# Seeding PSUM banks with ScalarE copies in the last layer of a two-layer transformer kernel

## The chip, the cores and the metric

One NeuronCore of a Trainium2 chip. The metric is the device time of one launch, in microseconds (us), of the slowest core, which here is the only one. TensorE multiplies matrices into PSUM (eight banks of 128 partitions by 512 float32). VectorE (DVE in the profile) and ScalarE (ACT) read and write PSUM and SBUF. GpSimd (POOL) works here on SBUF alone. The engines run in parallel, each through its own instruction stream in order, and wait for each other by semaphores.

## The reference

32 sequences of 128 tokens with 512 channels go through two layers. Layer 0 is attention with 16 heads of 64 and a mixture of eight experts. Layer 1, which the change concerns, is this:

```
normed = adaln(x, cond, w_adaln1, b_adaln1)          # layer norm, scale and shift from cond
q, k, v = normed @ wq.T + bq, normed @ wk.T + bk, normed @ wv.T + bv      # 16 heads of 32
attn = softmax(where(mask, -inf, q @ k.T / sqrt(32)))
x = x + (attn @ v) @ wo.T + bo
normed = adaln(x, cond, w_adaln2, b_adaln2)
h = gelu(normed @ w1.T + b1)                          # 512 -> 2048
x = x + h @ w2.T + b2                                 # 2048 -> 512
```

All in float32; shapes: x (32, 128, 512), wq, wk, wv, wo (512, 512), w1 (2048, 512), w2 (512, 2048).

## The kernel before

**Order of the work.** The kernel does not write its instructions in a fixed order. Every operation is handed to `Sched.op` (line 147) with an engine, a planned duration, a priority, the buffers that it reads and writes, and sometimes a second engine that could do it (`also`). `Sched.run` (line 193) then plans all engines together: it takes the operation that would leave its engine idle least, then the one of lowest priority number, and so fixes each engine's order once and for all when the program is built. The planned durations are in the functions at lines 299 to 316: 0.88 us for a product of the last layer, 0.68 us for a VectorE sum over 512 columns, 1.13 us for one on GpSimd, 0.62 us for a ScalarE copy. The helper `tt` (line 1199) hands in a sum of two tensors; unless its last argument is False, the planner may give it to VectorE (line 1201) or to GpSimd (line 1202).

**Seven products for eight.** All matrix products of layer 1 are done in Winograd's form of Strassen's algorithm: both operands are cut into quarters, seven products P1 to P7 of sums of quarters are made, and the four blocks of the result are

```
U2 = P1 + P6      U3 = U2 + P7      U4 = U2 + P5
C11 = P1 + P2     C12 = U4 + P3     C21 = U3 + P4     C22 = U3 + P5
```

The kernel works on groups of two sequences (`group`, line 2414) and on pairs G of groups (eight of them). In `group`, the q and k products (lines 2438 to 2481) write each of the seven P into a bank of its own; VectorE makes U2, U3, U4 and the four blocks from them, 512 columns at a time, and ScalarE takes P1 out of PSUM. The products for v and for the attention's output do the same in `seven_T` (line 2484) with 256 columns; the output's results are added to the residual x by VectorE (`onto_x`, `out_x`).

**The two levels of the MLP.** `up` (line 2667) makes h for a pair G and `down` (line 2742) the second product. Here the form is used twice: seven outer products in the order `ORDER` = 1, 2, 6, 7, 5, 4, 3, each made by seven inner ones in `inner` (line 2627). An inner product is four matmuls over 128x128 tiles. `inner` holds four banks: X collects P1, then P6, then P7 by accumulation, and ScalarE copies X out after each (`snap`, line 2641); Y takes P2, W takes P4, Z takes P5 and then P3. VectorE makes the four blocks with one sum each (`comb`, line 2645). Products of `up` carry m in the tile's name and those of `down` n, with the pair's number and the bank's letter: `m_3z` is bank Z of an inner product of `up` for G = 3.

In `up`, the outer sums U2, U3, U4 and the blocks of h are then made in SBUF by `add` (line 2684), four sums of 512 columns for each of the outer products 2, 6, 7, 4 and 3 and eight for 5, on either engine. Blocks of h go through the gelu on ScalarE (line 2693). In `down`, `form` and `sums` (line 2788) make the sums of quarters of h that the products need: 16 and 28 of 512 columns for each G, on either engine. They and the copies of the weights' pieces (`piece`, line 2617, on SyncE's queue) run ahead of the products by gates on `inner_done` and `stream`. The attention of the next two groups is planned in between the MLP of a pair.

**PSUM banks.** `bank` (line 342) is a new tile of the pool for each use; the planner counts eight.

Of the kernel before, what the change touches and what calls it, by code (L numbers as in the profile page):

```python
# [19 lines left out]
P = 128  # L20
# [30 lines left out]
class Buf:  # L51
# [3 lines left out]
    __slots__ = ("cls", "shape", "dtype", "name", "tile", "left", "end", "writers", "readers", "view")  # L55

    def __init__(self, cls, shape, dtype, name, tile=None):
        self.cls, self.shape, self.dtype, self.name, self.tile = cls, shape, dtype, name, tile
        self.left, self.end = 0, 0.0
        self.writers, self.readers = {}, {}  # L60
# [29 lines left out]
class Views:  # L90
# [36 lines left out]
    def give(self, at, b):  # L127
        self.free.append((at, b.view))

# [189 lines left out]
class Stage:  # L319


    def __init__(self, nc, ctx, tc, name, window, rows, smls, weights):
# [8 lines left out]
        self.views = Views(self.rows, self.weights)  # L331

# [9 lines left out]
    def bank(self, name, shape=(P, D)):  # L342
        return Buf(self.banks, list(shape), F32, name)

# [741 lines left out]
def fast_kernel(ctx: ExitStack, tc: tile.TileContext, x, condT, mask, cols, w_ada, wqkv, wout, wout_p, wout_o, wgate,  # L1086
# [86 lines left out]
    def transpose4(dst, src):  # L1173
        for c in range(4):
            nc.tensor.transpose(dst[:, c * P : (c + 1) * P], src[:, c * P : (c + 1) * P], ident)  # L1175
# [1158 lines left out]
    row = st.view  # L2334
# [26 lines left out]
    for i in (1, 2):  # L2361
# [7 lines left out]
    spun1 = bank("spun1")  # L2369
    sch.op(PE, 2.4, lambda: spin(22, spun1.t), w=[spun1], r=[pb0], prio=LB - 820.5, job=LJ)  # L2370

    dbq = const_tile("dbq", (P, 2))
    dbq_b = stands(dbq)
    sch.op(DVE, 0.16, lambda: nc.vector.tensor_tensor(
        dbq, prm[:, COL["bq"] + 2 : COL["bq"] + 4], prm[:, COL["bq"] : COL["bq"] + 2], ALU.subtract), w=[dbq_b], prio=900, job=5)
# [38 lines left out]
    def group(g):  # L2414
# [23 lines left out]
        ps = {m: bank(f"qk{m}_{g}", (P, 2, 2, S)) for m in range(1, 8)}  # L2438
        U1, U2, U3, U4 = (row(f"qu{m}_{g}", (P, 2, 2, S)) for m in "1234")

        def prod_qk(m, what, rhs, rr, ps=ps):
            for z, n in enumerate("qk"):
                w_, wb = l1w[n + what]

                def f_(z=z, w_=w_):
                    for u in range(2):
                        for k in range(2):
                            nc.tensor.matmul(ps[m].t[:, z, u, :], w_()[:, k, u * P : (u + 1) * P], rhs()[:, k, :],
                                             start=(k == 0), stop=(k == 1))
                sch.op(PE, mm_us(S, 4), f_, w=[(ps[m], z)], r=rr + [wb], prio=pp, job=job, keep=3)  # L2450

        def comb_qk(o_, a_, m, ps=ps):
            sch.op(DVE, dve_us(D), lambda: nc.vector.tensor_tensor(o_.t, a_.t, ps[m].t, ALU.add), w=[o_], r=[a_, ps[m]],
                   prio=pp, job=job)

        def first_qk(U1=U1, X=ps[1]):
            for u in range(2):
                nc.scalar.activation(U1.t[:, 0, u, :], X.t[:, 0, u, :], AF.Identity, bias=col("bq", u), scale=1.0)
            nc.scalar.copy(U1.t[:, 1, :, :], X.t[:, 1, :, :])

        def third_qk(U2=U2, U3=U3, X=ps[7]):
            for u in range(2):
                nc.vector.scalar_tensor_tensor(U3.t[:, 0, u, :], X.t[:, 0, u, :], dbq[:, u : u + 1], U2.t[:, 0, u, :],
                                               ALU.add, ALU.add)
            nc.vector.tensor_tensor(U3.t[:, 1, :, :], U2.t[:, 1, :, :], X.t[:, 1, :, :], ALU.add)

        prod_qk(1, "11", lambda: N_(1, 1), rN(1, 1))
        sch.op(ACT, 2 * act_us(S, 1) + act_us(QD), first_qk, w=[U1], r=[ps[1]], prio=pp - 1, job=job)
        prod_qk(2, "12", lambda: N_(2, 1), rN(2, 1))
        comb_qk(qk[1, 1], U1, 2)  # L2470
        prod_qk(6, "s2", lambda: NTv(2), [NTn[2]])
        comb_qk(U2, U1, 6)
        prod_qk(7, "s3", lambda: NTv(3), [NTn[3]])
        sch.op(DVE, 2 * dve_us(S, 1) + dve_us(QD), third_qk, w=[U3], r=[U2, ps[7], dbq_b], prio=pp, job=job)
        prod_qk(5, "s1", lambda: NTv(1), [NTn[1]])
        comb_qk(qk[2, 2], U3, 5)
        comb_qk(U4, U2, 5)
        prod_qk(4, "22", lambda: NTv(4), [NTn[4]])
        comb_qk(qk[2, 1], U3, 4)
        prod_qk(3, "s4", lambda: N_(2, 2), rN(2, 2))  # L2480
        comb_qk(qk[1, 2], U4, 3)
        v = [row(f"v_{g}_{i}") for i in range(GB)]

        def seven_T(n, Bn, rB, Tv, Tn, pr, first, comb, out2):

            ps = {m: bank(f"{n}{m}_{g}", (P, QD)) for m in range(1, 8)}
            U = {m: row(f"{n}u{m}_{g}", (P, QD)) for m in range(1, 5)}

            def prod(m, what, lhs, rr):
                w_, wb = l1w[n + what]  # L2490

                def f_():
                    for k in range(2):
                        nc.tensor.matmul(ps[m].t, lhs()[:, k, :], w_()[:, k, :], start=(k == 0), stop=(k == 1))
                sch.op(PE, mm_us(QD, 2), f_, w=[ps[m]], r=rr + [wb], prio=pr, job=job, keep=3)

            prod(1, "11", lambda: Bn(1, 1), rB(1, 1))
            sch.op(ACT, act_us(QD), lambda: nc.scalar.copy(U[1].t, ps[1].t), w=[U[1]], r=[ps[1]], prio=pr - 1, job=job)
            first(U[1], [(1, 1)])
            prod(2, "12", lambda: Bn(2, 1), rB(2, 1))  # L2500
            out2(1, 1, U[1], ps[2])
            prod(3, "s4", lambda: Bn(2, 2), rB(2, 2))
# [429 lines left out]
```

## Time and profile before

| what | value |
|---|---|
| three runs | 3350.45, 3350.43, 3348.22 us; median 3350.43 us |
| the profiled execution | 3349.9 us, span 3348.1 us, mean granted TensorE clock 0.983 |
| busy in the span | TensorE 3165.6 us (95%), VectorE 2642.0 (79%), GpSimd 1262.1 (38%), ScalarE 1060.6 (32%) |
| layer 1 | about 1907 us to the end |
| one pair G of layer 1 | 175.8 us from the first product of `down` of one G to that of the next |

The profile's page gives busy time by engine, the span in 40 slices and the costliest groups of instructions. Its rows name tiles as out<-in; `base` is a piece of a shared SBUF tile, so that most operands of layer 1 go by that name and must be told apart by line and shape. A float32 matmul shows as two records. The figure after `|` in a group's row is the engine's idle time just before the group and what ended it. A TensorE shown as busy is not one at its peak, since the records' ends are modelled; the distance from one start to the next tells the rate.

### The profile page before, as it was taken

The numbers are of one execution on the slowest core, as the hardware profiler recorded it, in microseconds if no ns is written. First come the engines' busy times: TensorE is split into PE (matmuls) and PEld (weight loads), VectorE is DVE, ScalarE is ACT, GpSimd is POOL, SyncE is SP. The second block draws the span as 40 slices with busy tenths as digits, with TensorE's granted clock in tenths as the row PEclk, the third lists the DMA queues.
The fourth block names the chain that finished last, engine by engine and source line by source line (L and its number), as shares of the span: only waits on it lengthen the run. The fifth ranks groups of instructions, "written<-read, shape, count | busy, mean of one in ns | idle before, by whom it ended". The sixth has DMA issues, their size and how long they took to land. (4 is left out here: it accounts for less than half of the span.)

```text
span 3348.1 us, 60612 instructions
## 1 busy us (share of the span) xinstructions
PE 3165.6 (95%) x22740; PEld 2563.1 (77%) x22740; DVE 2642.0 (79%) x5217; ACT 1060.6 (32%) x2613; POOL 1262.1 (38%) x939
## 2 busy tenths in 40 slices
PE   9999999999999999999999999898989898989887
PEld 5555555555568888888888898797979788888877
DVE  8877776888878876677555388888989888888887
ACT  3323332344330221222212124333333334342432
POOL 0322222221030456677665204334242515161625
PEclk9999999999999999999999999999999999999989
DMA  4243323453145433334333516445463535463655
GB/s 168 98 141 119 114 89 130 169 170 98 57 133 180 152 104 96 108 110 114 109 109 88 186 45 192 155 158 177 132 196 112 188 119 178 129 198 116 205 164 191
DMA packets 293455, 460.02 MB, mean 137 GB/s; under 512 B 29930, under 2 KB 111394, under 8 KB 293154
## 3 DMA queue, kind: packets, MB, share of 16 engines
q1 hardware_dynamic: 284498, 438.43, 40.1%
q0 software_dynamic: 7168, 16.91, 2.7%
q8 instruction: 183, 3.00, 0.4%
q14 instruction: 118, 0.97, 0.1%
q10 hardware_dynamic: 1488, 0.71, 0.1%
HBM read 383.44 MB, written 72.51 MB: 136 GB/s over the span
## 5 line engine op out<-in xcount | busy, mean ns | idle before, releaser
L1202 POOL TENSOR_TENSOR base<-base,base 128x512 f32<-128x512 f32 x324 | 462.6, 1442 | 695.5 <-DVE base L2645 273.9
L1201 DVE TENSOR_TENSOR base<-base,base 128x512 f32<-128x512 f32 (+2 forms) x657 | 508.4, 796 | 28.5 <-POOL base L1202 4.6
L2086 PE MATMUL d<-fc,h 128*128 128x256 f32 x992 | 218.9, 379 | 0.0
L2086 PEld LDWEIGHTS d<-fc,h 128*128 128x128 f32 x992 | 188.0, 190 | 25.3
L2033 ACT ACTIVATE h<-h,prm 128x256 f32<-128x256 f32 x256 | 115.0, 500 | 257.0 <-DVE h L2027 257.0
L2693 ACT ACTIVATE base<-base,prm 128x128 f32<-128x128 f32 x512 | 166.3, 394 | 53.2 <-DVE base L1201 39.4
L2022 PE MATMUL u<-gT,fc 128*128 128x256 f32 x768 | 178.7, 383 | 0.5 <-ACT gT L1985 0.5
L1389 ACT ACTIVATE sq<-qk 128x512 f32<-128x512 f32 x128 | 81.7, 638 | 295.3 <-DVE qk L1427 263.1
L2022 PEld LDWEIGHTS u<-gT,fc 128*128 128x128 f32 x768 | 147.4, 192 | 21.3 <-ACT gT L1985 0.9
L2027 DVE TENSOR_TENSOR h<-v,u 128x512 f32<-128x512 f32 x128 | 86.5, 683 | 49.1 <-PE u L2022 47.4
L2546 ACT ACTIVATE base<-sc,mbT 128x512 f32<-128x512 f32 x128 | 83.4, 687 | 121.5 <-PE sc L2543 73.6
L2022 PE MATMUL u<-tg,s 128*128 128x256 f32 x512 | 121.0, 379 | 0.9 <-DVE tg L1201 0.9
L2574 POOL TENSOR_TENSOR hi_t<-hi_t,base 128x512 f32<-128x512 f32 x32 | 41.8, 1306 | 206.6 <-DVE base L1212 202.2
L1423 PE MATMUL q<-wqkv,hsb 128*128 128x512 f32 x240 | 113.5, 595 | 0.0
L2086 PE MATMUL d<-t,hs 128*128 128x256 f32 x512 | 113.4, 379 | 0.0
L1423 PE MATMUL q<-t,hsa 128*128 128x512 f32 x240 | 112.9, 593 | 0.0
L1423 PE MATMUL q<-wqkv,hT 128*128 128x512 f32 x240 | 111.6, 598 | 0.2 <-DVE hT L1524 0.2
L2022 PEld LDWEIGHTS u<-tg,s 128*128 128x128 f32 x512 | 97.2, 190 | 14.4 <-issue 1.3
L2118 POOL DMA_INDIRECT acc<-y,idx x32 | 51.5, 1609 | 149.2 <-DVE y L2111 86.9
L2086 PEld LDWEIGHTS d<-t,hs 128*128 128x128 f32 x512 | 97.2, 190 | 13.2
L1391 DVE TENSOR_REDUCE var<-sq 128x8 f32<-128x512 f32 x128 | 86.4, 680 | 19.1 <-ACT sq L1389 18.1
L1175 PEld LDWEIGHTS tpq<-ident,qk 128*128 128x128 f32 x512 | 59.2, 142 | 50.1 <-issue 17.7
(1419 smaller groups left out, 8045.7 us busy)
## 6 DMA issues: line engine op xcount, KB each, us to landing
base<-w1i SPq DMA_DIRECT2D x224, 256.0 KB, 3.9
base<-w2i SPq DMA_DIRECT2D x224, 256.0 KB, 3.4
base<-w2s SPq DMA_DIRECT2D x168, 256.0 KB, 3.9
fc<-in_fc_dram SPq DMA_DIRECT2D x64, 512.0 KB, 4.6
fc<-in_fc_dram SPq DMA_DIRECT2D x32, 1024.0 KB, 5.5
base<-w1s SPq DMA_DIRECT2D x96, 256.0 KB, 3.6
base<-in_w_dram SPq DMA_DIRECT2D x72, 256.0 KB, 4.8
x<-in_x_dram SPq DMA_DIRECT2D x32, 256.0 KB, 3.3
```

Of the source, the lines that this page charges most:

```text
L1175: nc.tensor.transpose(dst[:, c * P : (c + 1) * P], src[:, c * P : (c + 1) * P], ident)
L1201: ways = {DVE: (DVE, dve_us(n), lambda: nc.vector.tensor_tensor(o_(), a_(), b_(), op_)), POOL: (POOL, pool_us(n), lambda: nc.gpsimd.tensor ...
L1202: POOL: (POOL, pool_us(n), lambda: nc.gpsimd.tensor_tensor(o_(), a_(), b_(), op_))}
L1389: sch.op(ACT, act_us(D), lambda: nc.scalar.activation(sq.t, qk[i][j].t, AF.Square), w=[sq], r=[qk[i][j]], prio=pr, job=job)
L1391: sch.op(DVE, dve_us(D), lambda: nc.vector.tensor_reduce(var[i].t[:, j * 8 : (j + 1) * 8], sq.t, AX.X, ALU.add), w=[(var[i], j)], r=[sq], ...
L1423: nc.tensor.matmul(ps[m].t, lhs()[:, k, :], rhs[0](k), start=(k == 0), stop=(k == 1))
L2022: nc.tensor.matmul(ps[n].t[:, t, :], lhs()[:, k, t * P : (t + 1) * P], rhs.t[:, k, :], start=(k == 0), stop=(k == 1))
L2027: sch.op(DVE, dve_us(D), lambda: nc.vector.tensor_tensor(o_.t, a_.t, ps[n].t, ALU.add), w=[o_], r=[a_, ps[n]], prio=pr, job=job)
L2033: sch.op(ACT, act_us(HQ, 1), lambda t=t, c=c: nc.scalar.activation(o_.t[:, t, :], o_.t[:, t, :], AF.Gelu_apprx_tanh, bias=col("b1s", e * 1 ...
L2086: nc.tensor.matmul(ps[n].t[:, j, :], lhs[m].t[:, k, t * P : (t + 1) * P], rhs.t[:, 2 * m + k, :], start=(m == 0 and k == 0), stop=(m == NM ...
L2546: sch.op(ACT, act_us(D, 1), lambda sc=scs[r], pe=pe[r], b=b: nc.scalar.activation(pe.t, sc.t, AF.Exp, bias=mbT[:, b : b + 1], scale=sm1), ...
L2693: sch.op(ACT, act_us(S, 1), lambda k=k, u=u, c=c: nc.scalar.activation(o_[k].t[:, u * S : (u + 1) * S], o_[k].t[:, u * S : (u + 1) * S], A ...
```

## The change

**MLP, up.** `inner` is renamed `chained` and stays for `down`. `up` gets `seeded`, with three banks and another order of the products (P1, P5, P6, P2, P7, P3, P4):

- X takes P1. ScalarE copies X into bank Y, a PSUM bank, and TensorE adds P2 onto it: Y is C11.
- X takes P6 and is U2. ScalarE copies it into bank Z (after copying P5 out of Z into t_, in SBUF), and TensorE adds P3 onto it.
- X takes P7 and is U3; VectorE adds t_ (P5) to it: C22. X then takes P4 and is C21. VectorE adds t_ to Z: C12.

For outer product 1, Y isn't seeded (P1 goes to SBUF, VectorE adds it to P2). The outer sums onto C11 and C21 are made by VectorE straight out of PSUM, in the instruction that takes the block out; those onto C12 and C22 stay sums in SBUF (`onto`), on GpSimd, or on either engine for outer products 4 and 3.

**q, k, v and the attention's output.** The seven banks become three in the same manner. For q and k ScalarE adds the bias as it copies; two of the four blocks leave PSUM by ScalarE, one by VectorE with P5 added, one likewise in three instructions. For v, ScalarE copies P1, U2, P5 and one block out; VectorE makes the other three. For the output, VectorE adds every intermediate to x directly out of PSUM, with eight sums for eleven.

**down.** `sums` is now for GpSimd alone (`NFORM` is False). Its products are as before.

**Banks.** `held_bank` keeps the eight PSUM tiles as long as the program lasts and reuses them; a bank is marked full when matmuls have written all of its 512 columns, and only such a bank may be seeded. The matmuls of transposes, scores and the attention's output set their start flag on the first of a bank alone.

```diff
+    def seeded(name, shape, mm, lhs_of, piece_of, dest, pr, job, new):
+        X, Z = (bank(f"{name}{c}", shape) for c in "xz")
+        Y, t_ = bank(f"{name}y", shape, not new), row(f"{name}t", shape)
...
+        def copied(o_, src):
+            sch.op(ACT, act_us(n), lambda: nc.scalar.copy(o_.t, src.t), w=[o_], r=[src], prio=pr - 3000, job=job)
+
+        prod(X, 1, True, 4, w=[begun], r=gate + ([] if new else [Y]))
+        prod(Z, 5, True, 1)
+        if new:
+            u_ = row(f"{name}u", shape)
+            copied(u_, X)
+        else:
+            copied(Y, X)
+        prod(X, 6, False, 0)
+        copied(t_, Z)
+        prod(Y, 2, new, 0)
+        copied(Z, X)
+        dest((1, 1), Y, u_ if new else None)
+        prod(X, 7, False, 0, w=[go])
+        prod(Z, 3, False, 0)
+        dest((2, 2), X, t_)
+        prod(X, 4, False, 0)
+        dest((1, 2), Z, t_)
+        dest((2, 1), X, None)
...
+            first, plus = {1: (None, None), 2: (q1, None), 6: (q1, None), 7: (uu, None), 5: (u3, uu), 4: (u3, None), 3: (uu, None)}[o]
+            def dest(blk, src, t_, first=first, plus=plus, d_=d_, po=po, o=o):
+                k = BLK.index(blk)
+                if t_ is None:
+                    if first is None:
+                        sch.op(ACT, act_us(D), lambda: nc.scalar.copy(d_[k].t, flat(src)), w=[d_[k]], r=[src], prio=po - 2990, job=job)
+                        return
+                    sch.op(DVE, dve_us(D), lambda: nc.vector.tensor_tensor(d_[k].t, flat(src), first[k].t, ALU.add),
+                           w=[d_[k]], r=[src, first[k]], prio=po - 2990, job=job)
+                    if plus:
+                        sch.op(DVE, dve_us(D), lambda: nc.vector.tensor_tensor(plus[k].t, flat(src), plus[k].t, ALU.add),
+                               w=[plus[k]], r=[src, plus[k]], prio=po - 2990, job=job)
+                    return
+                sch.op(DVE, dve_us(D), lambda: nc.vector.tensor_tensor(d_[k].t, flat(src), flat(t_), ALU.add),
+                       w=[d_[k]], r=[src, t_], prio=po - 3000, job=job)
+                if plus:
+                    onto(plus, d_, k, po)
+                if first:
+                    onto(d_, first, k, po, POOL, o in (4, 3))
...
-            elif o == 5:
-                add(uu, H["22"], 5, po)
-                add(H["22"], u3, 5, po)
...
+        prod_qk(X, "11", lambda: N_(1, 1), rN(1, 1), True, 3, [Y])
+        prod_qk(Z, "s1", lambda: NTv(1), [NTn[1]], True, 1)
+        biased(Y, X, 1, pp - 2)
+        prod_qk(X, "s2", lambda: NTv(2), [NTn[2]], False)
+        copied(t_, Z, pp - 1)
+        prod_qk(Y, "12", lambda: N_(2, 1), rN(2, 1), False)
+        biased(Z, X, 1, pp - 2)
+        prod_qk(X, "s3", lambda: NTv(3), [NTn[3]], False)
+        copied(qk[1, 1], Y, pp)
+        prod_qk(Z, "s4", lambda: N_(2, 2), rN(2, 2), False)
+        sch.op(DVE, 2 * dve_us(S, 1) + dve_us(QD), out22, w=[qk[2, 2]], r=[X, t_], prio=pp, job=job)
+        prod_qk(X, "22", lambda: NTv(4), [NTn[4]], False)
+        sch.op(DVE, dve_us(D), lambda: nc.vector.tensor_tensor(qk[1, 2].t, Z.t, t_.t, ALU.add), w=[qk[1, 2]], r=[Z, t_], prio=pp, job=job)
+        biased(qk[2, 1], X, 2, pp)
...
+            prod(X, "11", lambda: Bn(1, 1), rB(1, 1))
+            prod(Z, "s1", lambda: Tv(1), [Tn[1]], keep=2)
+            once(1, X)
+            prod(Y, "12", lambda: Bn(2, 1), rB(2, 1), keep=1)
+            once(5, Z)
+            prod(X, "s2", lambda: Tv(2), [Tn[2]], False, 0)
+            after(1, 1, Y)
+            once(2, X)
+            prod(Z, "s4", lambda: Bn(2, 2), rB(2, 2), False, 0)
+            prod(X, "s3", lambda: Tv(3), [Tn[3]], False, 0)
+            after(1, 2, Z)
+            once(3, X)
+            prod(W, "22", lambda: Tv(4), [Tn[4]], W is not X, 0)
+            after(2, 1, W)
...
-                    tt(o_[0], a_[0], b_[0], op_, D, [o_[1]], [a_[1], b_[1], *(inner_done[-2:-1] if z > 1 else inner_done[-5:-4])], po - 3, job, POOL)
+                    tt(o_[0], a_[0], b_[0], op_, D, [o_[1]], [a_[1], b_[1], *(inner_done[-2:-1] if z > 1 else inner_done[-5:-4])], po - 3, job, POOL, NFORM)
```

## The prediction

> **What bounds the kernel now.** I read the page first: TensorE is busy 95% of the span, so time can come only from its gaps and from stretches at a lower clock. Then busy time by stretch for one repeat of layer 1 (first product of `down` for G = 3 to that for G = 4: `down`, then `up`) and for the last G:
>
> ```profile
> core 0: us, PE busy (x) PEld busy (x) DVE busy (x) ACT busy (x) POOL busy (x), PEclk, DMA share, GB/s
> 2600.60:2679.70 79.10, 67.52 (x655) 62.11 (x654) 67.81 (x119) 30.44 (x81) 40.59 (x29) 0.94 0.57 184
> 2679.70:2776.40 96.70, 93.38 (x791) 88.02 (x790) 86.30 (x184) 33.66 (x82) 24.68 (x18) 1.00 0.43 140
> 3206.80:3278.70 71.90, 59.46 (x497) 55.03 (x496) 58.68 (x113) 27.38 (x64) 25.83 (x19) 0.88 0.56 183
> 3278.70:3339.40 60.70, 49.74 (x410) 47.77 (x408) 45.62 (x67) 16.14 (x57) 32.48 (x23) 0.94 0.59 183
> ```
>
> VectorE is as full as TensorE: 67.8 + 86.3 = 154.1 us of 175.8. `up` (second line) is nearly dense on TensorE; `down` is not, and its granted clock falls to 0.94. TensorE's own need in a repeat, from distances between starts where it runs dense: 98 MLP products x 0.893 us = 87.5; q and k 14 x 1.79 = 25.0; v and output 28 x 0.87 = 24.4; transposes 8 x 0.89 = 7.1; scores 4 x 1.1 = 4.4; exp sums and attention outputs 8 x 0.87 = 7.0. Sum 155.4, so 20.4 us of a repeat are lost.
>
> TensorE's waits in the same repeat say where:
>
> ```profile
> engine line waited for: us in total, times, longest us
> PE n_3z L2754 <- issue: 5.9, 3, 5.2
> PE a_8t L1175 <- DVE base L2384: 2.8, 2, 2.6
> PE m_4w L2681 <- ACT base L2396: 1.3, 1, 1.3
> PE o L2494 <- DVE base L1201: 1.1, 2, 0.9
> PE n_3z L2754 <- POOL base L1202: 1.0, 1, 1.0
> PE qk L2448 <- DVE base L1201: 0.8, 1, 0.8
> PE a_11t L1175 <- DVE base L2384: 0.6, 1, 0.6
> ```
>
> With smaller ones they make 14.9 us. The rest is clock, as TensorE's timeline at the longest wait shows:
>
> ```profile
> 2616.24 1.17 PE L2543 MATMUL sc<-base 32*128 32x128 f32 x32
> 2622.65 2.05 PE L2754 MATMUL n_3z<-base,base 128*128 128x128 f32 x8 [5.24 <-issue]
> 2625.15 2.05 PE L2754 MATMUL n_3z<-base,base 128*128 128x128 f32 x8 [0.45 <-issue]
> 2626.99 1.46 PE L2754 MATMUL n_3y<-base,base 128*128 128x128 f32 x8
> ```
>
> After 5.24 us idle a product takes 2.05 us, not 1.06. "issue" names nobody, but the timelines of the others do: from 2613.5 to 2622.4 VectorE makes six sums in 8.86 us and GpSimd seven in 11.32. These are `form` and `sums` for outer product 6 of `down`: the last block of h needs its outer sum, its gelu, then three sums in a row before this product can start.
>
> Last, VectorE's groups in the repeat:
>
> ```profile
> L1201 DVE TENSOR_TENSOR base<-base,base 128x512 f32<-128x512 f32 x40 | 42.6, 1085 | 2.5 <-PE m_4w L2681 0.8 <-POOL base L1202 0.6 <-ACT base L2693 0.2
> ...
> L2453 DVE TENSOR_TENSOR base<-base,qk 128x512 f32<-128x512 f32 x12 | 7.8, 683 | 0.2
> ```
>
> The same sum costs 1085 ns with both inputs in SBUF and 683 ns with one in PSUM.
>
> **The change part by part, for one repeat.**
>
> *MLP sums.* VectorE's 28 block sums in `up` (681 ns each, line 2645) become 29: 27 out of PSUM plus two for outer product 5, +0.7 us. Of `add`'s 28 SBUF sums 14 stay, ten on GpSimd alone. `form`'s 16 may go to either engine; `sums`' 28 go to GpSimd. VectorE keeps 11 SBUF sums that only it can make; I give it 12 of the 20 free ones: 23 for 40. GpSimd: 38 forced + 8 = 46 for 43.
>
> A rule speaks here. The row says 17 x 1.085 = 18.4 us off VectorE. The Trainium skill, "SBUF — State Buffer", section Who interferes with whom, says that a VectorE instruction with two SBUF inputs and a GpSimd instruction that reads SBUF exclude each other for the whole instruction. The trace agrees: the norm's 128x2 steps, 0.16 us alone, take 1.12 to 1.18 us three times ahead of a_8t, with GpSimd at work. By the rule the port counts: GpSimd's sums hold it about 1.27 us (its shortest), VectorE's about 0.62 (estimate: 0.68, the shortest in the trace, less overlap). Before 43 x 1.27 + 40 x 0.62 = 79.4 us, after 46 x 1.27 + 23 x 0.62 = 72.7: only 6.7 us freed. So pinning `sums` to GpSimd gives part of the gain back. I take VectorE's 18.4 us as real in `up`, and for the chains in `down`, where both work, only a part.
>
> *q and k.* Off VectorE per group: seven results (six of 0.683, one of 2 x 0.346 + 0.412) for two, -3.4 us; x 2 groups = -6.8. Added on ScalarE: two bias copies of 2 x 0.363 + 0.372 = 1.1 and two copies of 0.58, +3.4, x 2 = +6.7.
> *v.* Four VectorE sums fewer (0.416), three ScalarE copies more (0.372): -3.3 and +2.2.
> *Output.* Eleven VectorE sums to eight, and four of them change from SBUF (0.51) to PSUM (0.418): -3.3 us; ScalarE -0.7.
> *Totals.* VectorE 154 - 31 = 123 us of 175.8 (70%). ScalarE 64 + 8.8 (with one copy more in outer product 1) = 73. TensorE unchanged: products, transposes and their flags are the same number of instructions. DMAs and SyncE's queue: none added or moved; weights are gated by products and follow them.
>
> *ScalarE writing PSUM* is in no row. Nearest is its 512-column copy from PSUM to SBUF, 0.582 us, which I take; ends: 0.37 (its 256-column row) and 0.69 (its 512-column exp). A seed in PSUM needs no extra matmul in the diff.
>
> *New waits.* P6 waits for the copy of X, with P5 alone between; P7 waits for the copy of U2, with P2 between. From the first matmul's start a product ends at 1.06 us by its records, ScalarE starts 0.04 later, copies 0.58, TensorE follows 0.05 later: 1.73. The cover ends at 2 x 0.893 = 1.79. It holds by 0.06 us when ScalarE is free, and not when a gelu piece (0.39) is ahead in its queue; behind TensorE's waiting product stands everything else. `inner` already had P6, P4, P7 with the same cover, and `up` runs dense. P6's place can also hold the former inner product's P4. I charge 1.0 us per repeat (0.02 for each of 49); if the cover is gone, 0.3 each, 15 us. P4 waits for VectorE to read X, with P3 and mostly the next P1 between.
>
> *What it is worth on TensorE, per repeat.*
> - The 5.9 us wait and the half clock after it (6.8 us, 2.1 of them idle: 2.4 lost): C11 and C21 of the last outer product save one SBUF sum each (1.27), three chained sums go from 1.48 to about 1.0 (1.4), and half of the clock loss follows: 4.0. Next late are the same sums, now on GpSimd.
> - a_8t: the output chain has three 0.42 us sums fewer ahead of the norm: 1.2. The norm's small steps stay late.
> - q, k and a_11t, 1.7 us in all with small ones, wait for VectorE in `up`: 1.2.
> - m_4w waits for a bank; fewer banks are taken: 0.7.
> - o and n_3z behind GpSimd: 0. New waits: -1.0.
>
> Sum 6.1, x 7 repeats = 43. The last G has no attention to fill in: waits of 23.2 us and some 8 us of clock (12% of 71.9 us and 6% of 60.7, about a third of it idle), of which the same two chains save 40%: 12. Before G = 0, some 7 us of idle: 3. In all 58.
>
> The profiled execution took 3349.9 us, 0.5 below the median, so 3349.9 - 58 = 3292, and about the same beside the median.
>
> **The rivals.**
>
> *VectorE was the bound, and nearly all waits go.* For: its 154 us against TensorE's 155. A repeat would lose 6 us for 20.4: 7 x 14 = 100, and 25 at the ends: 3225. Against: the waits in `down` are chains of dependent sums, and no freer engine shortens gelu or GpSimd.
>
> *The gain is eaten by tight covers.* ScalarE's gelu pieces delay the copies, 0.1 us on average at each of 49 places: 5 us per repeat, 4 more than charged, x 8 = 32: 3324.
>
> *GpSimd becomes the bound of `down`; slower.* Four sums for each outer product at 1.455 us (its mean) = 5.8 us, against seven products in 6.25. It decides from 1.56 us per sum. At 1.9 us, 7.6 - 6.25 = 1.35 late for each of 56 outer products: 76 us lost against 58 gained: 3368. For: the pinned sums, and the rule above. Against: attention adds to TensorE's time in `down` (79.1 us for seven outer products, so 11.3 each), and VectorE has fewer two-input sums there.
>
> *The change only moves the waits.* The planner's durations (0.68 for a sum that takes 1.085) make a new order with new mishaps: 3348.
>
> **How the numbers follow.** What a measurement of this kernel can tell from no change is about 0.2%, 6.7 us. Forecast, 3265 to 3325: 0.56. VectorE the bound, 3225: 0.16. Covers, 3324: 0.14. Moved waits: 0.06. GpSimd the bound: 0.08. Faster 0.86, same 0.06, slower 0.08. The slow case lies outside the range with half of the first rival's case: 3220 to 3346.
>
> **What would show it.** Right: VectorE below 130 us a repeat; about 23 two-input 512-column sums on it; products of `up` still 0.893 us apart; a repeat of about 169.5 us; the long wait before outer product 6 below 4 us. Wrong: TensorE waiting for ScalarE copies in `up`; many waits of n tiles for GpSimd; GpSimd's mean above 1.56 us; an unchanged 5 us wait.

## The result, and the profile after

The changed kernel takes 3302.77 us (median of four runs, 3301.14 to 3306.21) against 3350.44 us for the kernel before in the same comparison: ratio 0.9858, 95% interval 0.9841 to 0.9875. It is 47.7 us faster; 58 was forecast. The profiled execution took 3301.1 us, with a span of 3299.4 against 3348.1.

Where the 48.7 us of span came from is read off the starts of the first products of `up` and `down` for each G:

| stretch | before | after | gained | forecast |
|---|---|---|---|---|
| start to the first product of `down`, G = 0 | 2075.4 | 2073.5 | 1.9 | 3 |
| six repeats, `down` G to `down` G + 1 | 1053.0 | 1016.9 | 36.1 | 43 (7 x 6.1), with the next line |
| `down` of the seventh, G = 6 | 78.4 | 72.6 | 5.8 | |
| last `up` and last `down` | 132.6 | 128.6 | 4.0 | 12 |
| after the last product | 8.7 | 7.9 | 0.8 | 0 |

Busy time by stretch, for the same four stretches as before (`down` and `up` of the repeat, then of the last G); the columns are named by the first line:

```profile
core 0: us, PE busy (x) PEld busy (x) DVE busy (x) ACT busy (x) POOL busy (x), PEclk, DMA share, GB/s
2581.60:2654.30 72.70, 64.41 (x639) 59.30 (x638) 56.12 (x102) 25.43 (x67) 42.86 (x31) 0.95 0.59 185
2654.30:2751.30 97.00, 95.02 (x808) 90.16 (x805) 72.23 (x165) 46.95 (x114) 20.58 (x16) 1.00 0.47 150
3163.00:3235.70 72.70, 61.21 (x515) 57.23 (x512) 54.31 (x105) 32.59 (x75) 20.61 (x16) 0.88 0.60 187
3235.70:3291.60 55.90, 48.07 (x402) 46.63 (x400) 34.55 (x56) 12.70 (x46) 40.41 (x29) 0.97 0.60 192
```

By these stretches the whole gain of a repeat is in `down`, 79.1 to 72.7 us, and `up`, which was dense, stays at 97 although VectorE does 14 us less there. In part that is where the cut falls: two products of 0.893 us now stand in the second stretch and no longer in the first (PE shows 639 and 808 records for 655 and 791, eight to a product). For equal work `down` gained about 4.6 us and `up` about 1.5. The last `up` holds two products more as well and goes from 71.9 to 72.7; the last `down` falls from 60.7 to 55.9 with one fewer. VectorE is down to 56.12 + 72.23 = 128.4 us a repeat.

TensorE's waits in the repeat (line, what it waited for, us in all, times, longest):

```profile
PE bank L2867 <- POOL base L1266: 5.7, 2, 3.9
PE bank L2785 <- ACT bank L2746: 1.8, 2, 1.1
PE bank L2553 <- DVE base L1265: 0.9, 2, 0.6
PE bank L2867 <- DVE base L2712: 0.9, 2, 0.5
PE bank L2609 <- DVE base L2712: 0.4, 1, 0.4
PE bank L2867 <- ACT base L2708: 0.2, 1, 0.2
```

They make 9.9 us, where all waits before made 14.9. All PSUM tiles of layer 1 are now called `bank`, so they are told apart by line: 2785 is a product of `up`, 2867 of `down`, 2609 a score, 2553 a product of v or of the output, 1238 a transpose. Of the releasers, 1265 and 1266 are the sums of `tt` on VectorE and GpSimd, 2712 VectorE's block sums in `down`, 2746 and 2708 ScalarE's copies out of a bank in `up` and `down`. The transposes' wait for the norm (2.8 + 0.6 us before) is gone, and so are q's and k's and the bank wait of `up`. The long wait is still there, shorter and with a name. TensorE's timeline around it:

```profile
2593.21 2.05 PE L2867 MATMUL bank<-base,base 128*128 128x128 f32 x16 [0.52 <-DVE base L2712]
2595.71 1.17 PE L2609 MATMUL bank<-base 32*128 32x128 f32 x32 [0.45 <-DVE base L2712]
2600.80 3.75 PE L2867 MATMUL bank<-base,base 128*128 128x128 f32 x16 [3.91 <-POOL base L1266]
2604.34 1.80 PE L2867 MATMUL bank<-base 128*128 128x128 f32 x8
```

It was 5.24 us and is 3.91, and the products after it still take 1.77 us each (from 2600.80 to 2604.34 two of them), not 0.893. The granted clock (third figure from the end) is half behind this wait in both kernels. Before, it was half a second time, behind the transposes' wait:

```profile
2621.10:2627.70 6.60, 4.60 (x20) 4.37 (x21) 6.50 (x10) 1.79 (x4) 3.32 (x4) 0.50 0.21 65
2665.50:2668.70 3.20, 3.20 (x17) 3.20 (x16) 2.15 (x7) 1.14 (x3) 0.51 (x1) 0.50 0.39 118
2599.20:2605.80 6.60, 5.00 (x23) 5.03 (x24) 6.53 (x8) 1.54 (x3) 5.35 (x4) 0.50 0.25 79
```

The first two lines are of the kernel before, the third of the changed one. In the traces' clock records these stretches last 6.83, 3.41 and 6.83 us. What TensorE waits for is the last of these sums of GpSimd, made while VectorE makes sums of its own:

```profile
2595.00 4.95 POOL L1266 TENSOR_TENSOR base<-base,base 128x512 f32<-128x512 f32 x3 [0.69 <-DVE base L1265]
2595.58 4.92 DVE L1265 TENSOR_TENSOR base<-base,base 128x512 f32<-128x512 f32 x3
```

Last the groups of the repeat that hold the sums and the new copies:

```profile
L1265 DVE TENSOR_TENSOR base<-base,base 128x512 f32<-128x512 f32 x25 | 26.8, 1086 | 2.2 <-ACT base L2795 1.4
L1266 POOL TENSOR_TENSOR base<-base,base 128x512 f32<-128x512 f32 x41 | 55.8, 1377 | 88.8 <-DVE base L2836 49.0 <-PE bank L2867 18.6 <-DVE base L1265 12.2
L2746 ACT COPY bank<-bank 128x512 f32<-128x512 f32 x13 | 7.4, 572 | 7.3 <-PE bank L2785 6.0 <-ACT base L2795 0.7 <-DVE a_11t L423 0.3
L2746 ACT COPY base<-bank 128x512 f32<-128x512 f32 x8 | 4.7, 586 | 6.9 <-PE bank L2785 5.4 <-DVE base L1265 1.6
```

VectorE's two-input SBUF sums fell from 40 to 25 at an unchanged mean. The third line is the seeding: a ScalarE copy from one PSUM bank into another.

### The profile page after: what moved, and what is told of

Its sections match the earlier page's. It is cut to its first block, busy times and chain, and to the rows that moved or that the text cites. A ratio compares the mean times of both kernels' runs of the same rounds, so it can differ in the third digit from the quotient of the medians.

```text
span 3299.4 us, 60330 instructions
## 1 busy us (share of the span) xinstructions
PE 3154.7 (96%) x22740; PEld 2560.1 (78%) x22740; DVE 2438.3 (74%) x4913; ACT 1127.9 (34%) x2777; POOL 1254.2 (38%) x950
## 4 chain that ended last, share of the span: by engine, by line
PE 78%; DVE 11%; issue 2%; POOL 2%; DMA 1%; ACT 1%; SPq 0%; DVEq 0%; another core or an unknown queue 0%; ACTq 0%; POOLq 0%
PE d L2150 12%; PE u L2086 12%; PE bank L2785 10%; PE q L1487 8%; PE bank L2867 8%; PE bank L2508 6%; PE w L1738 5%; PE bank L2553 5%; PE v L1487 3%; DVE base L1265 2%; POOL base L1266 2%; PE po L1662 1%; PE sc L1640 1%; PE tpq L1238 1%; PE bank L2621 1%
## 5 line engine op out<-in xcount | busy, mean ns | idle before, releaser
L1266 POOL TENSOR_TENSOR base<-base,base 128x512 f32<-128x512 f32 x336 | 455.7, 1372 | 660.7 <-DVE base L2836 353.9
L2867 PE MATMUL bank<-base,base 128*128 128x128 f32 x3048 | 382.8, 285 | 55.6 <-POOL base L1266 43.6
L2867 PEld LDWEIGHTS bank<-base,base 128*128 128x128 f32 x3048 | 366.5, 199 | 68.3 <-POOL base L1266 46.0
L1265 DVE TENSOR_TENSOR base<-base,base 128x256 f32<-128x256 f32 (+2 forms) x469 | 372.2, 811 | 27.6 <-ACT base L2795 11.5
L2785 PE MATMUL bank<-base,base 128*128 128x128 f32 x3080 | 372.5, 279 | 19.1 <-ACT bank L2746 14.7
L2785 PEld LDWEIGHTS bank<-base,base 128*128 128x128 f32 x3080 | 361.8, 193 | 28.6 <-ACT bank L2746 18.3
L2712 DVE TENSOR_TENSOR base<-base,bank 128x128 f32<-128x128 f32 x224 | 58.4, 281 | 115.2 <-PE bank L2867 47.9
L2708 ACT COPY base<-bank 128x128 f32<-128x128 f32 x168 | 44.5, 265 | 243.6 <-PE bank L2867 240.2
```

The costliest lines, as they stand in the source:

```text
L1265: ways = {DVE: (DVE, dve_us(n), lambda: nc.vector.tensor_tensor(o_(), a_(), b_(), op_)), POOL: (POOL, pool_us(n), lambda: nc.gpsimd.tensor ...
L1266: POOL: (POOL, pool_us(n), lambda: nc.gpsimd.tensor_tensor(o_(), a_(), b_(), op_))}
L2785: nc.tensor.matmul(b_.t[:, u, :], w_.t[:, u * P : (u + 1) * P], x_(), start=fresh and u == 0, stop=True, skip_group_check=True)
L2867: nc.tensor.matmul(b_.t, x_()[:, k * S : (k + 1) * S], w_.t[:, k, :], start=fresh and k == 0, stop=True, skip_group_check=True)
```

## The experiments

The ratios are to the kernel before, with 95% intervals.

| kernel | median us | ratio |
|---|---|---|
| before | 3350.44 | 1 |
| after | 3302.77 | 0.9858 [0.9841, 0.9875] |
| e1: `sums` free to use either engine | 3310.95 | 0.9886 [0.987, 0.9903] |
| e2: `up` as before, attention changed | 3356.47 | 1.0017 [1.0007, 1.0027] |
| e3: attention as before, `up` changed | 3322.05 | 0.9926 [0.9909, 0.9942] |
| e4: before, with `sums` on GpSimd | 3350.63 | 1.0001 [0.9995, 1.0008] |
| e5: outer sums of `up` in SBUF again | 3354.52 | 1.0014 [1.0007, 1.002] |
| e6: the same for outer product 3 alone | 3312.68 | 0.9887 [0.987, 0.9903] |
| e7: 7 more VectorE instructions a repeat | 3302.13 | 0.9858 [0.9842, 0.9875] |
| e8: range check planned later | 3302.65 | 0.9859 [0.9842, 0.9875] |
| e9: 49 more VectorE instructions a repeat | 3383.35 | 1.0099 [1.0083, 1.0116] |
| e10: four `form` sums of later priority | 3306.73 | 0.9869 [0.9852, 0.9885] |
| e11: held banks alone | 3365.16 | 1.0044 [1.0029, 1.0058] |
| e12: after, bank freed longest ago first | 3292.24 | 0.9826 [0.9813, 0.984] |

### e1 to e4: which part of the change pays

The first question was which of the three parts carries the gain, and whether pinning `sums` to GpSimd costs something, as the prediction held.

**e1**, the changed kernel with the pin undone:

```diff
-    NFORM = False
+    NFORM = True
```

> The changed kernel, but the sums of quarters in down may again go to VectorE or GpSimd. Theory A (the pinning gives part of the gain back[...]): the 3.9 us wait for GpSimd before outer product 6 falls to about 2, a repeat from 169.4 to about 168, 3292. Theory B (the pinning is a part of the gain: it keeps VectorE free for what only VectorE can do): VectorE back to about 140 us a repeat, a repeat of 172, 3320.

Measured 3310.95: 8 us slower, half of what the second theory had. The pin helps here; the sign that the prediction gave it was wrong. A repeat takes 170.7 us in the mean, with VectorE at 133 us. In `down` of the repeat from G = 3 it shows 60.3 us for 56.1 (first line). That repeat itself took only 0.2 us longer than in the changed kernel, so TensorE's waits are shown over the whole of layer 1:

```profile
2589.80:2662.10 72.30, 64.54 (x639) 59.29 (x637) 60.33 (x108) 25.27 (x67) 35.56 (x25) 0.95 0.59 188
PE bank L2867 <- DVE base L2712: 29.8, 22, 3.4
PE bank L2867 <- POOL base L1266: 24.4, 14, 2.2
```

In the changed kernel these two are 8.9 and 43.6 us (shown under e12). The wait for GpSimd's sums is nearly halved, but a longer one for VectorE's block sums has appeared. A likely reading is that VectorE, with more sums of `down` on it, comes late to read a bank; no run of e1 with another choice of banks tests it.

**e2** puts the old `up` back (seven inner products with `chained`, outer sums by `add`), **e3** the old q, k, v and output. Both keep the held banks and the pin.

```diff
e2:
-            seeded(f"m{o}_{G}", (P, 4, S), mm, lhs_of, piece_of, dest, po, job, o == ORDER[0])
+            chained(f"m{o}_{G}", (P, 4, S), mm, lhs_of, piece_of, dest, po, job)
...
e3:
-        X, Z, Y = (bank(f"qk{c}_{g}", (P, 2, 2, S), c == "y") for c in "xzy")
-        t_ = row(f"qt_{g}", (P, 2, 2, S))
+        ps = {m: bank(f"qk{m}_{g}", (P, 2, 2, S)) for m in range(1, 8)}
+        U1, U2, U3, U4 = (row(f"qu{m}_{g}", (P, 2, 2, S)) for m in "1234")
...
```

> The changed kernel, but up has its four-bank form and its separate outer sums again; q, k, v, output, banks and the pinned sums as changed. Theory A (the gain comes mostly from up: fewer SBUF sums and a shorter chain to the last gelu): 5 of the 6.4 us per repeat go, 3340. Theory B (VectorE's total busy time is what counts, and up gives 18 of the 26 us saved per repeat): 4.4 us per repeat go, 3334. Theory C (the attention part is the source): 3312.

> The changed kernel, but q, k, v and the output's products have their seven banks and VectorE sums again. Theory A (up is the source): 1.5 us per repeat are lost, the waits of q, k and transposes in up come back, 3314. Theory B (VectorE's total time: 13 of the 31 us planned saving): 2.7 us per repeat, 3323. Theory C (the attention part is the source): 3340.

**e4** is the kernel before with the pin alone:

```diff
-                    tt(o_[0], ..., po - 3, job, POOL)
+                    tt(o_[0], ..., po - 3, job, POOL, False)
```

> The kernel before, with the one change that the sums of quarters in down go to GpSimd alone. Theory A (pinning costs): GpSimd's waits in down grow by 1 to 2 us per repeat, 3360. Theory B (pinning is a part of the gain): VectorE loses some 12 sums a repeat, 3335.

Without the new `up` nothing is left of the gain (3356.5, 6 us slower than before, and beyond all three theories; the twelve runs lie in two groups, four at 3346.6 to 3349.6 and eight at 3355.3 to 3359.1). With the new `up` and the old attention 28 of 48 us remain; this is where the theory of VectorE's total time had put it (3323). The pin alone does nothing to the time, though it takes the transposes' 2.8 us wait away: in the same repeat products of `down` then wait 5.8 us for GpSimd, where they waited 1.0. So `up` carries the gain, and the attention's part is worth 19 us beside the new `up`, though 6 are lost when attention, held banks and pin come without it. The two parts don't add.

### e5 and e6: fewer VectorE instructions, or shorter chains

Of the parts of `up`, the outer sums looked decisive: onto C11 and C21 they come straight out of PSUM in the new kernel. **e5** keeps the seeding, but takes these blocks out by ScalarE and makes the outer sum in SBUF with `onto`. **e6** does so for outer product 3, the last, alone (`o == 3`).

```diff
+                if t_ is None and first and o > 0:
+                    sch.op(ACT, act_us(D), lambda: nc.scalar.copy(d_[k].t, flat(src)), w=[d_[k]], r=[src], prio=po - 2990, job=job)
+                    if plus:
+                        onto(plus, d_, k, po)
+                    onto(d_, first, k, po, POOL, o in (4, 3))
+                    return
```

> The changed kernel, but in up the blocks C11 and C21 are copied out of PSUM by ScalarE and get their outer sums afterwards in SBUF, as C12 and C22 do: 14 VectorE sums fewer per pair G, 14 sums more that go to GpSimd (or, for outer products 4 and 3, to either engine), 12 ScalarE copies more. Theory A (what pays is the shorter way from the last products of up to the last gelu): each of these blocks comes about 1.2 us later and GpSimd has more to do, 3303 to about 3330. Theory B (what pays is VectorE's total busy time, which falls by some 9 us per repeat here): 3290 to 3303.

> As the run with separate outer sums, but for outer product 3 alone, the last of up: 2 of the 14. Theory A (it is the way to the last gelu): at least half of that run's loss, 3315. Theory B (number of SBUF sums and port time): 2/14 of it, 3304 to 3307.

e5 loses everything (3354.5), far more than either theory had. e6 costs 10 us, a fifth of e5's 52: the theory of the way to the last gelu had asked for half, that of the number of sums for a seventh. The stretches of e5's repeat:

```profile
2604.60:2680.80 76.20, 65.42 (x638) 59.68 (x636) 57.75 (x101) 27.77 (x76) 44.78 (x32) 0.96 0.56 174
2680.80:2781.20 100.40, 95.71 (x808) 90.37 (x805) 70.69 (x155) 50.59 (x118) 34.42 (x26) 1.00 0.46 147
```

VectorE is busy 57.75 + 70.69 = 128.4 us, as in the changed kernel, and yet the repeat is 7 us longer, half of it in `up`. So 128 us of VectorE are not what makes the kernel fast. What moved is GpSimd's work in `up`, 20.6 to 34.4 us, with one more link in the chain from a product to a block of h. TensorE's waits tell a part of it (line numbers behind an edit shift: 2873 is the product of `down` here):

```profile
PE bank L2873 <- POOL base L1266: 6.4, 3, 4.2
PE bank L2785 <- ACT bank L2746: 4.5, 4, 1.3
```

Against 5.7 and 1.8 that is 3.4 of the 7 us; with its smaller entries the list grows from 9.9 to 15.1 us. ScalarE's part of it, 2.7 us, is at the end of `up`, where this happens three times:

```profile
2765.04 13.02 POOL L1266 TENSOR_TENSOR base<-base,base 128x512 f32<-128x512 f32 x9
2774.75 0.69 ACT L2795 ACTIVATE base<-base,prm 128x128 f32<-128x128 f32 x2 [2.01 <-POOL base L1266]
2775.35 0.57 ACT L2746 COPY bank<-bank 128x512 f32<-128x512 f32 x1
2775.98 2.05 PE L2785 MATMUL bank<-base,base 128*128 128x128 f32 x16 [1.32 <-ACT bank L2746]
```

GpSimd makes nine sums there without a gap. A gelu step (line 2795) waits for it, the copy that seeds a bank comes behind that step in ScalarE's order, and TensorE waits for the copy. In the changed kernel TensorE waits there once, 1.1 us. So within `up` it is GpSimd's queue, by way of ScalarE's, that e5 pays for. For `down`, e5 doesn't divide the loss between added copies, added sums and a longer chain.

### e7 and e9: is VectorE's time worth anything?

A filler instruction reads one 512-column row and writes a small tile that nothing uses; it runs once (**e7**) or seven times (**e9**) for each outer product of `up`, that is 7 or 49 times a repeat.

```diff
         dest((2, 2), X, t_)
+        fill = sml(f"{name}fill", 6)
+        for _ in range(7):                      # e7: once
+            sch.op(DVE, dve_us(D), lambda: nc.vector.bn_stats(fill.t, flat(t_)), w=[fill], r=[t_], prio=pr, job=job)
```

> The changed kernel, and one more VectorE instruction per inner product of up (statistics over 512 columns of t_, result unused, 0.68 us, one SBUF input), 49 a repeat, 33 us: VectorE at about 161 us, above the 154 of the kernel before. Theory A (chains count, not the total): 3303 to 3315. Theory B (VectorE's room is what pays): the gain goes, 3345 or more.

`seeded` is called once for an outer product, not once for each inner one, so the 49 times and 33 us of that text are wrong: the group shows seven.

```profile
L2764 DVE BATCH_NORM_STATS2 m_4fill<-base 128x6 f32<-128x512 f32 x7 | 4.7, 685 | 1.8 <-ACT base L2746 1.8
```

At 4.7 us a repeat the time is the same, 3302.13 us, and so are the waits. It took e9 to add what had been meant.

> The changed kernel, and seven more VectorE instructions (statistics over 512 columns of t_, result unused, 0.68 us each) in each of the seven calls that make an outer product of up. The run with one in each had 7 a repeat and not 49, so only 4.7 us; this one has 49, 33 us: VectorE at about 161 us of a repeat, above the 154 of the kernel before. Theory A (chains count, not the total): 3303 to 3320. Theory B (VectorE's room is what pays): the gain goes, 3345 or more.

e9 costs 80.6 us (3383.35 - 3302.77), at about 178.7 us a repeat; the gain is gone, as the theory of VectorE's room had it. But VectorE is not at 161 us. The first line is e9's repeat, 153.9 us on VectorE; then its two-input sums of 512 columns from the first product of `down` to the end, in e9 and in the changed kernel:

```profile
2614.22:2793.67 179.45, 161.63 (x1441) 151.02 (x1441) 153.86 (x310) 71.78 (x177) 74.42 (x55) 0.97 0.51 156
L1265 DVE TENSOR_TENSOR base<-base,base 128x512 f32<-128x512 f32 x134 | 150.7, 1149 | 8.8 <-POOL base L1266 5.9 <-PE bank L2870 1.2
L1265 DVE TENSOR_TENSOR base<-base,base 128x512 f32<-128x512 f32 x199 | 215.0, 1096 | 17.2 <-ACT base L2795 11.5
```

The planner moved 65 sums away; GpSimd makes 390 of them for 322, and 74.4 us of a repeat for 63.4. So e9 fills VectorE to what it had in the kernel before (154.1) and loads GpSimd as well. Over layer 1 TensorE's largest waits are now

```profile
PE bank L1238 <- DVE base L2444: 27.4, 8, 4.4
PE bank L2609 <- ACT base L2613: 26.1, 8, 5.1
PE bank L2870 <- POOL base L1266: 25.8, 14, 9.6
PE bank L2621 <- DVE base L2712: 14.3, 6, 2.9
```

The transposes' wait for the norm is back (first line). Up to 132 us a repeat (e7) more load on VectorE costs nothing. With 154 us, in a plan that puts more on GpSimd too, the new form has no gain left. Where between the two VectorE's load begins to cost, and what GpSimd's share of the 80.6 us is, no run tells.

### e8: the range check at the end

In the last `up` TensorE waits 4.0 us for the norm, then 2.9 and 2.2 us for steps of the range check of h's inputs (lines 2952 to 2954):

```profile
PE bank L1238 <- DVE base L2444: 4.0, 1, 4.0
PE bank L2953 <- DVE fok L2952: 2.9, 1, 2.9
PE bank L2785 <- DVE fok L2954: 2.2, 1, 2.2
```

**e8** plans that check later.

```diff
-        sch.op(eng, us, fn, w=w_, r=r_, prio=LB + (NG4 - 1) * 1000.0 + 190, job=fl)
+        sch.op(eng, us, fn, w=w_, r=r_, prio=LB + (NG4 - 1) * 1000.0 + 1140, job=fl)
```

> The changed kernel, but the eight small steps of the range check at the end (VectorE and one tiny matmul) get a later priority, between up and down of the last G, so that TensorE no longer waits 2.85 us for them in its order within the last up. If this wait and the 2.2 us after it are what kept the last G from gaining more than 4 us: 3297, with more granted clock in the last up. If the last up waits for its norm anyway: 3303.

No difference: 3302.65, as the second of the two expectations had it. The last `up` is 1.5 us shorter (71.2), but a wait that the changed kernel hadn't stands in the place of the check's, the second line here:

```profile
PE bank L1238 <- DVE base L2444: 4.0, 1, 4.0
PE bank L2785 <- DVE base L1265: 3.9, 1, 3.9
PE bank L2867 <- POOL base L1266: 3.9, 1, 3.9
```

The last `up` has no other work to put into its gaps, and taking one stall away uncovers the next.

### e10: sums moved in the plan

**e10** gave four sums of `form` (one call, for one quarter) a later priority, to reach the 3.9 us wait.

```diff
-            form(a21, a11, a21, ALU.subtract, pr - 900)
+            form(a21, a11, a21, ALU.subtract, pr - 0.5)
```

> The changed kernel, but in down the four sums of form that only outer product 7 needs (a21) get a later priority than those that outer product 6 needs. Theory A (the 3.9 us wait before outer product 6 is the chain of sums behind the last gelu, and other sums stand between its links): the wait falls by two sums, 2 us, and with less half clock after it 2 to 3 us a repeat, 3280 to 3290. Rival (the links wait for the gelu, and sums between them fill time that is idle anyway): 3303.

The order of instructions is the changed kernel's on every engine. So it is a repeat of the changed kernel, 3306.73 us and 0.9869 [0.9852, 0.9885], and says nothing of the chain. It does show how far two measurements of one program lie apart: 4 us. In the profiled executions the distance lies ahead of the first product of `down` (2079.8 us for 2073.5); a repeat takes 169.4 us for 169.5.

### e11 and e12: the held banks

**e11** has the old `up`, the old attention and free `sums`: of the change only the held banks, with the start flags that go with them, are left.

> The changed kernel's held banks and start flags with all products in the form of before and the sums of quarters free for both engines: banks alone. If reusing the bank that was freed last costs waits (theory of bank reuse: it explains why attention in the new form with up in the old one was 6 us slower than before): 3356. If banks are neutral and the new attention form costs when up is as before: 3350.

3365.16 us: the held banks by themselves cost 14 us, where the theory had 6. In layer 1 each engine makes the same operations on the same shapes in the same order as in the kernel before, so it is where the tiles lie that costs. In TensorE's waits over layer 1, transposes stand behind VectorE's block sums of `down` (line 2714 in this kernel), whose results they don't read. The kernel before has no such entry in its list. Products of `up` stand behind the block sums of `up` itself (same line, 512 columns), with 15.8 us for 7.5 before:

```profile
PE bank L1238 <- DVE base L2714: 17.9, 6, 3.0
PE bank L2787 <- DVE base L2714: 15.8, 24, 2.9
```

What a transpose needs of a block sum is its bank. `held_bank` gives out the bank that was freed last, by the plan; if VectorE runs a little behind the plan, its reader is still at work. **e12** is the changed kernel with that choice turned round:

```diff
-        best = max(good, key=lambda x: (not x[2], x[0]))
+        best = max(good, key=lambda x: (not x[2], -x[0]))
```

> The changed kernel with one choice of the bank allocator turned round: among banks that are equally good it takes the one freed longest ago instead of the one freed last. Theory (a product often waits for VectorE because it is given the bank that VectorE has only just read): the waits of TensorE for the n block sums of VectorE (L2712), 12.1 us over this layer's window in the changed kernel, mostly vanish, and the time is about 3290 to 3295. Rival (those waits are for data, or another order of banks only moves the wait to another instruction): the waits change their names, their sum stays within 3 us, and the time stays at 3303 give or take 5. The waits of n products for GpSimd's sums (L1266, 43.6 us over the layer) should be unchanged under both.

3292.24 us: 10.5 us less than the changed kernel, with intervals that just don't overlap; the fastest version of all. Line by line each engine has the same order of instructions as in the changed kernel's trace, so nothing but the bank each tile lies in is different. From the first product of `down` to the last, e12 is 8.5 us shorter. TensorE's waits over layer 1 that are concerned, first of the changed kernel, then of e12:

```profile
PE bank L2867 <- POOL base L1266: 43.6, 15, 3.9
PE bank L2867 <- DVE base L2712: 8.9, 17, 1.7
PE bank L2609 <- DVE base L2712: 3.2, 7, 0.5
PE bank L2867 <- ACT base L2708: 1.5, 7, 0.2
```

```profile
PE bank L2867 <- POOL base L1266: 45.2, 15, 5.4
PE bank L2609 <- DVE base L2712: 5.8, 7, 0.9
PE bank L2867 <- ACT base L2708: 5.4, 7, 0.8
```

The wait of products of `down` for block sums is gone. By this list alone the rival would have been right about the sum: others grew, and these lines together fell by 0.8 us, the whole list by 1.9. But the list counts from the modelled end of a matmul, which lies later than the next one could have started. Counted from start to start instead, the distances of 0.26 us and more between TensorE's matmuls, from the first product of `down` on, exceed the usual 0.112 us by 135.2 us in the changed kernel and by 126.5 in e12: 8.7 us, about the 8.5 by which the two differ. So the time did come from short stalls, and the list of waits undercounts them.

## Why the prediction was right, and where it was not

**The place and the size: right.** Seven repeats were to give 43 us and gave 41.9; most of it is in `down`, and `up` stayed dense. VectorE was to fall below 130 us a repeat: 128.4, where the working had 123. About 23 two-input sums on it: 25. ScalarE 73: 72.4. A repeat of 169.5 us: 1016.9 / 6 = 169.5. That it came out to a tenth is luck, as its terms show.

**The terms inside a repeat: two mis-sized, in opposite directions.** They are counted here from start to start of TensorE's matmuls, as under e12, with the distances at half clock:

| us of TensorE lost in the repeat to | before | after | gained | forecast |
|---|---|---|---|---|
| the long wait, slow products behind it, waits for banks just ahead of it | 8.3 | 7.8 | 0.5 | 4.0 |
| the transposes' wait and slow products behind it | 4.7 | 0.2 | 4.5 | 1.2 |
| the other wait for GpSimd | 1.2 | 1.9 | -0.8 | 0 |
| all else (q, k, banks in `up`, output, ScalarE's copies) | | | 1.9 | 0.9 |
| sum | | | 6.1 | 6.1 |

The long wait itself did what was forecast, 5.24 to 3.91, below 4 and now behind GpSimd's sums. But half of the clock loss did not follow: the clock is at half for 6.83 us as before. The wait with the slow products lost 8.3 us and loses 6.5, and two waits for banks just ahead of it (0.52 and 0.45 by the list, 1.3 from start to start) are new.

The step "the norm's small steps stay late" was wrong the other way. The transposes' wait of 2.8 us is gone whole, and with it the second stretch at half clock, 3.41 us, which the prediction didn't count. A part of this is only moved: a product just ahead of the transposes waits 1.77 us for GpSimd, where such a wait was 1.02, and the norm is done at 2641.46, just as the transposes start (2641.52). The shorter output chain, which the prediction gave as the reason, isn't needed: e4 doesn't have it and loses this wait too. In e9, with VectorE at 154 us, such waits come to 27.4 us over layer 1, so VectorE's load has a part in them. The right sum hid two terms that were each off by over 2 us.

**New waits: the count was wrong.** "0.02 for each of 49" took every inner product for a place with a tight cover. The tight places, P6 and P7, come once for each outer product, 14 a repeat. TensorE waits for ScalarE's copies there 1.8 us in two places; 1.0 had been charged. The rival of tight covers (3324) rested on the same 49. With the 1.3 us of bank waits named above, the new waits cost three times the charge.

**Held banks: missing.** The prediction took "fewer banks are taken" for a gain of 0.7 us and nothing else. The rule by which banks are reused costs 10.5 us (e12), spread over all of layer 1. That this is about the whole distance between forecast and result is chance: the repeats reached their forecast with this cost in them, and 8 of the 10 us that are short are short in the last G.

**The last G: the term that was most mis-sized.** 12 us forecast, 4.0 measured. "The same two chains save 40%" did not hold: the waits of the last G fell from 23.2 us to 19.1 by the list. In the last `up` the wait for the norm is 4.0 us, where it was 1.7, and the range check follows with 2.9 + 2.2. That stage became 0.8 us longer, though with two products more in it, and e8 shows that removing one of its stalls only brings the next. The last `down` gave 4.8.

**The rule of the Trainium skill.** "SBUF — State Buffer", section Who interferes with whom, was weighed as speaking against the pin. As a rule the trace bears it out: where both engines make sums at once, three take 4.95 us on GpSimd and 4.92 on VectorE, 1.64 each, against 1.27 and 0.68 at their shortest; all six are done 5.5 us after the first began, where the rule with the prediction's 1.27 + 0.62 makes 5.7. What was drawn from it was wrong: the pin gives nothing back. Undoing it costs 8 us (e1), and pinning alone costs nothing (e4). The waits of e1 suggest why: a sum on VectorE stands ahead of block sums that must clear a bank, and TensorE then waits for those.

**The rivals.** *VectorE was the bound* falls in its simple form: e5 has the same VectorE time and none of the gain, and e7 adds to it for nothing. Its grain of truth is that the room must be there: e9 takes it away and the gain with it, and e3 came out where VectorE's total put it. *The gain is eaten by tight covers* does not hold in the changed kernel (1.8 us a repeat), but it is what happens in `up` of e5. *GpSimd the bound of `down`* fell by its own threshold, 1.412 us a sum in `down` (27 sums in 37.8 us) against 1.56; still, 43.6 us of layer 1's waits now stand behind GpSimd, the largest entry that is left. *The change only moves the waits* holds for the last `up` and in part for products of `down`, not for the repeat.

**What did the gain come from, then?** Shown: the gain needs the new `up` (e2), and within it the outer sums taken straight out of PSUM instead of through SBUF (e5, of which the last outer product is a fifth, e6); the attention's part adds to that (e3). Room on VectorE goes with it (e9) but is not enough (e5). Read from the trace: in `up`, e5 loses by GpSimd's longer queue, which holds up the gelu and with it ScalarE's seeding copies. Not shown: what the shorter chain from the last product to the last block of h is worth by itself, since e5 and e6 lengthen that chain and GpSimd's queue together. An experiment that puts the outer sums of e5 on VectorE, with its load held constant, wasn't run; nor were e2 and e3 with the bank choice of e12, so how much of their losses is the held banks stays open.

## What to carry to other kernels

When sums are taken off a busy engine, ask which chain of dependent steps gets shorter and which queue the sums join: here equal busy time on VectorE went with 3302.8 us and with 3354.5. Before a filler is read as a load on one engine, count what the planner moved to make room for it (e9). When buffers are reused by a plan, try giving out the one that has been free longest, not the one freed last; here that one character was worth 10.5 us beside the 47.7 of the whole change. And a stall at the end of a program, where there is nothing to fill it, can be worth less than its length, since the next stall stands behind it (e8).

## What the runs showed of the hardware

ScalarE copies 512 columns from PSUM into PSUM in 572 ns and into SBUF in 586: seeding a bank costs no more than a copy out. After 3.91 us idle TensorE still fell to half its rate, 1.77 us a product for 0.893, with the granted clock at half for 6.83 us as after 5.24 us idle: the shortened wait saved its own length and nothing of the clock behind it. Sums of GpSimd and VectorE that overlap take 1.64 us each, six of them 5.5 us: 0.92 us a sum for the two engines together. VectorE with GpSimd idle makes one in 0.69 us (at 2576.32, 2577.72, 2581.80 and 2583.20 of the changed kernel), so in that stretch the two finished fewer sums than VectorE makes by itself in the same time; its 1.086 us is a mean over both cases. And from the recorded end of a GpSimd sum to the product that waited for it 0.52 or 0.85 us pass (15 waits of the changed kernel; GpSimd's recorded spans are rough), after a block sum of VectorE 0.05.
